# The table of expert blocks, made one piece earlier behind each layer

## The chip, the cores and the metric

The kernel runs on one core of one Trainium2 chip. The metric is the device time of one execution in microseconds (us), and less is better. Several executions are timed and their median is taken; one further execution is recorded by the hardware profiler, and its time is given beside its span.

## The reference

The input is a batch of 8 sequences of 512 tokens with 256 features, all in float32. Four sublayers follow each other, each added to its input behind a layer norm:

```python
x = x + scan_layer(layernorm(x))       # Win, silu, decaying state, Wout
x = x + mixture(layernorm(x))          # 16 routed experts + shared expert
x = x + attention(layernorm(x))        # 16 heads, causal, scores clipped to +-10
x = x + mixture(layernorm(x))          # the same mixture again
```

The mixture is what the change touches. The router gives each token 16 scores (a sigmoid). The 16 experts form 4 groups; the 2 best groups are kept, and in them the 4 best experts. Their weights are normalised and scaled by 2.5. A token's output is the weighted sum of its 4 experts, each `silu(x @ gate) * (x @ up) @ down` with 256 inner features, plus a shared expert of twice that width, which all tokens pass.

## The kernel before

The work has four stages in this order: a stretch for the scan layer, the routed experts of the first mixture, a stretch for attention, and the routed experts of the second mixture.

**A stretch** (`stretch(layer)`) loops over the 8 sequences. Beside the layer's own matmuls for a sequence b it routes sequence b-1 (`Route`: norm, transposes and scores, `choices`) and computes the shared expert of sequence b-2 (`shared_experts`). `choices` is a long chain of small VectorE (DVE) operations: it picks the experts (L558 to L602), counts tokens by expert with two small TensorE (PE) matmuls (`pr`, L609 and L610), works out a row number in DRAM for each choice (L614 to L635) and the weights (L639 to L642), and sends each token's row to its places with 16 indirect DMAs on GpSimd (POOL, L656) into `xg`, where each of the 16 experts has a region of its own.

**Two closing pieces** follow the loop, since routing and shared experts lag behind. The first piece holds the rest of the shared expert of sequence 5 and all of sequence 6's, with the routing of sequence 7. The second holds the shared expert of sequence 7 and the last 8 sends. In a shared expert, L902 is a gate or up matmul (tile `pg`), L919 (first mixture) or L915 (second) its activation on ScalarE (ACT), L920 and L921, or L916 and L917, the two DVE products that make `act`, L930 the down matmul (tile `pd`), L938 its copy out of PSUM on ACT, and L939 its store.

**The table** (`blocks(i, table)`) is what turns the counts into a list of blocks of 128 rows that all belong to one expert. It is a generator of five steps:

1. the regions' ends go to integers (`ends`, L675), SyncE (SP) loads them into registers (L676), and 16 DMAs write zeros behind the regions (L684);
2. the number of blocks by expert, and their sum (`n`, `more`, `nb`, `total`, `many`, L687 to L698);
3. the place of each candidate block in the list (`has`, `ahead`, `also`, `at`, L706 to L717);
4. a 0/1 matrix `chosen` (L721, 128 x 572);
5. 4 + 4 + 4 matmuls that read `chosen` (`pe`, L732, and twice `pl`, L741), a copy on ACT (`expert`, L736), and DVE operations that write the addresses as integers (`spare`, `lines`, L745, L749, L752).

**The routed experts** (`routed`) read the table: each engine loads block addresses from `lines` into registers, SP loads a block's 128 rows (L787), PE transposes them (L802), runs gate and up (`ph`, L813) and down (`pyr`, L841), and POOL adds the rows to the output with an indirect DMA (L850). 136 blocks run in each of the two stages; a branch for more is not taken.

**What sets the order.** `beside(...)` merges several pieces by a share of progress: it always takes a step from the piece that has come the least way. `timed(steps, *places)` gives steps fixed places between 0 and 1 of the merged piece, and after the last place runs what is left of the generator. `spread(a, b, n)` gives n even places. A scheduler then reorders somewhat, so that places are a request and the built order decides; each engine executes its own instructions strictly in the built order, and waits for semaphores.

**PSUM.** In the scan stretch there are 8 banks for all matmul outputs; in the attention stretch 4 for everything but the attention scores (`banks_of(one=4, pair=2)`). A new tile waits until the bank's former tile has been read.

Of the kernel before, what the change touches and what calls it, by code (L numbers as in the profile page):

```python
# [72 lines left out]
def tile_hybrid_block(  # L73
# [61 lines left out]
    def rows_of(part, b: int):  # L135
        return part[b * T : (b + 1) * T, :].rearrange("(t p) d -> p t d", p=P)
# [191 lines left out]
    def timed(steps, *places):  # L328


        def scaled():
            now = 0
            for place in places:
                yield place - now
                now = place
                next(steps)
            for _ in steps:
                pass

        return Piece(1, scaled())  # L340

    def spread(first: float, last: float, many: int):
        return [first + (last - first) * k / many for k in range(many)]

    def some(steps, many: int):

        for _ in range(many):
            yield next(steps)

    def issue(piece):  # L350
        for _ in piece.steps:
            pass


    def turned(src, tag: str, into, copies, home=None):

        rows = src()
        if home is None:
            dst = work.tile([P, KD, T], FP, tag="kb4", name=f"xT_{tag}", bufs=KB)
        else:  # L360
            dst = home(f"xT_{tag}")
        into(dst)
        for k in range(KD):
            pt = bank([P, NT, P], f"pt_{tag}_{k}")
            for t in range(NT):
                nc.tensor.transpose(pt[:, t, :], rows[:, t, k * P : (k + 1) * P], ident)
            flat = pt.rearrange("p t q -> p (t q)")
            copies[k](dst[:, k, :], flat)
            yield T // 2
# [4 lines left out]
    def normed(b: int, tag: str, place, by_vector: bool = False):  # L374

        x_sb = x_tiles[b]
        stats = small.tile([P, NT, 6], FP, tag="stats", name=f"stats_{tag}")
        mv = small.tile([P, NT, 2], FP, tag="mv", name=f"mv_{tag}")
        for t in range(NT):
            nc.vector.bn_stats(stats[:, t, :], x_sb[:, t, :])  # L380
            nc.vector.bn_aggr(mv[:, t, :], stats[:, t, :])
            yield
        rstd = small.tile([P, NT], FP, tag="rstd", name=f"rstd_{tag}")
        if by_vector:


            var = small.tile([P, NT], FP, tag="var", name=f"var_{tag}", bufs=1)
            nc.vector.tensor_scalar(var, mv[:, :, 1], EPS, None, ALU.add)
            bits = small.tile([P, NT], I32, tag="bits", name=f"bits_{tag}", bufs=1)
            nc.vector.tensor_scalar(bits, var.bitcast(I32), 1, None, ALU.logical_shift_right)  # L390
            nc.vector.tensor_scalar(rstd.bitcast(I32), bits, -1.0, HALVED, ALU.mult, ALU.add)
            off = small.tile([P, NT], FP, tag="off", name=f"off_{tag}", bufs=1)
            for _ in range(3):
                nc.vector.tensor_mul(off, rstd, rstd)
                nc.vector.scalar_tensor_tensor(off, off, -0.5, var, ALU.mult, ALU.mult)
                nc.vector.scalar_tensor_tensor(rstd, off, 1.5, rstd, ALU.add, ALU.mult)
            yield
        else:
            nc.vector.tensor_scalar(rstd, mv[:, :, 1], EPS, None, ALU.add)
            nc.gpsimd.tensor_tensor(rstd, rstd, neg_half, ALU.pow)  # L400
        xn = place()
        for t in range(NT):
            nc.vector.tensor_scalar(
                xn[:, t, :], x_sb[:, t, :], mv[:, t, 0:1], rstd[:, t : t + 1], ALU.subtract, ALU.mult
            )
            yield

    def kb4(name: str):
        return work.tile([P, NT, D], FP, tag="kb4", name=name, bufs=KB)
# [762 lines left out]
    def stretch(layer):  # L1172


        i = layer.mixture
        xT, xn, made, routes, sends = {}, {}, {}, {}, []

        def norm(b: int):
            def place():
                xn[b] = kb4(f"xn_{i}_{b}")  # L1180
                return xn[b]

            return normed(b, f"l{i}_{b}", place)

        def turn(b: int):
            return turned(lambda: xn.pop(b), f"l{i}_{b}", lambda xnT: xT.update({b: xnT}), layer.copies)

        def project(b: int):
            made[b], piece = layer.project(b, xT.pop(b))
            return piece  # L1190

        def store(b: int):
            nc.sync.dma_start(out=rows_of(parts[i][0], b), in_=x_tiles[b])

        def experts(b: int):
            return shared_experts(i, b, lambda: routes.pop(b).held["xnT"], i == 1)

        for b in range(layer.ahead):
            if b < layer.early:
                xT[b] = ready.pop(b)  # L1200
            else:
                layer.load(b)
                issue(Piece(0, norm(b)))
                issue(Piece(0, turn(b)))
            if b == 0:
                issue(project(b))
        def start_route(b: int):
            routes[b] = Route(i, b, layer.copies)
            store(b)
            return routes[b]  # L1210

        for b in range(B):
            pieces = [layer.main(b, made.pop(b))]
            nxt, last = b + layer.ahead, b == B - 1
            fill = []
            if layer.ahead > 1 and not last:
                fill.append(project(b + 1))
            if b > 1:
                shared_sum = experts(b - 2)
                if last:  # L1220

                    each = shared_sum.columns // 12
                    rest = Piece((12 - HELD) * each, shared_sum.steps)
                    shared_sum = Piece(HELD * each, some(shared_sum.steps, HELD))
                fill.append(shared_sum)
                pieces.append(timed(sends.pop(), 0.1, 0.14, 0.18, *spread(0.22, 0.66 if last else 0.86, NT * TK)))
            if fill:
                pieces.append(behind(*fill))
            if b > 0:
                r = start_route(b - 1)  # L1230
                pieces.append(timed(r.norm(), *spread(0.0, 0.12, NT), *spread(0.2, 0.28, NT)))
                sends.append(r.rest)
                if last:
                    pieces += [
                        timed(r.scores(), 0.35, 0.38, *spread(0.45, 0.5, NT)),
                        timed(some(r.rest, PICKS), *spread(0.52, 0.66, PICKS)),
                        timed(some(r.rest, 3 + SENT), 0.69, 0.71, 0.73, *spread(0.75, 1.0, SENT)),
                    ]
                else:
                    pieces += [  # L1240
                        timed(r.scores(), 0.42, 0.46, *spread(0.55, 0.6, NT)),
                        timed(some(r.rest, PICKS), *spread(0.66, 0.95, PICKS)),
                    ]
            if nxt < B:
                layer.load(nxt)
                pieces += [
                    timed(norm(nxt), *spread(0.32, 0.44, NT), *spread(0.56, 0.64, NT)),
                    timed(turn(nxt), 0.75, 0.79),
                ]
            issue(beside(*pieces))  # L1250
            if layer.ahead == 1 and nxt < B:
                issue(project(nxt))
        layer.end()

        r = start_route(B - 1)
        chain = 3 + PICKS
        issue(
            beside(  # L1260
                behind(rest, experts(B - 2)),
                timed(r.norm(by_vector=True), *spread(0.0, 0.05, 2 * NT)),
                timed(sends.pop(), *spread(0.0, 0.5, NT * TK - SENT)),
                timed(r.scores(), 0.2, 0.22, *spread(0.28, 0.33, NT)),
                timed(some(r.rest, chain + 8), *spread(0.36, 0.68, chain), *spread(0.7, 1.0, 8)),
            )
        )
        table = []
        issue(
            beside(  # L1270
                experts(B - 1),
                timed(r.rest, *spread(0.0, 0.5, NT * TK - 8)),
                timed(blocks(i, table), 0.03, 0.14, 0.26, 0.38),
            )
        )
        return table

    with banks_of(one=8):
        table = stretch(Scan())
        wqkv_sb, wo_sb = load_attention_weights()  # L1280
# [6 lines left out]
    with banks_of(one=4, pair=2):  # L1287
        table = stretch(Attention())
# [82 lines left out]
```

## Time and profile before

| | |
|---|---|
| median of 3 executions | 1802.87 us (1798.23 to 1807.11) |
| profiled execution: time | 1817.59 us |
| profiled execution: span | 1815.9 us, mean granted PE clock 0.965 |
| PE busy | 1694.6 us, 93% |
| DVE busy | 1088.1 us, 60% |
| ACT busy | 805.3 us, 44% |
| POOL busy | 763.0 us, 42% |
| first closing pieces (scan) | about 321 to 385 us of the span |
| first routed experts | from about 385 to 795 us |
| second closing pieces (attention) | about 1310 to 1377 us |
| second routed experts | about 1377 us to the end |

The span runs from the first to the last instruction of the profiled execution. A row of the timeline gives start, duration, engine, source line, operation, tiles and count; a bracket holds the idle time of that engine just before and what ended it. Matmuls are recorded twice each here, so 2 matmuls are x4. A wait for several semaphores is put down to the one that came last. A few matmul records can be missing, and their ends are modelled.

### The profile page before, as it was taken

Reading aid. Unit: us, or ns where it says so; the run is one execution under the profiler, and the core shown is the slowest. Engines: PE = TensorE matmul, PEld = TensorE weight load, DVE = VectorE, ACT = ScalarE, POOL = GpSimd, SP = SyncE. Lnnn points to the kernel's source line nnn. Section 1 sums busy time; section 2 is a strip of 40 time slices with the busy share of each in tenths; the row PEclk is TensorE's granted clock in tenths of the full one; section 3 lists DMA queues with packets and bytes.
Section 4 is the critical chain, followed back from the end, with each engine's and each line's share of the span. In section 5 each row is a group of like instructions: output and inputs, shape, how many; then the busy total and the mean of one; then the engine's idle time right before and its main releaser. Section 6 shows DMA issues by size and latency. Waiting matters only on the chain. (4 is left out here: it accounts for less than half of the span.)

```text
span 1815.9 us, 32773 instructions
## 1 busy us (share of the span) xinstructions
PE 1694.6 (93%) x10640; PEld 1264.8 (70%) x10640; DVE 1088.1 (60%) x3364; ACT 805.3 (44%) x1740; POOL 763.0 (42%) x665
## 2 busy tenths in 40 slices
PE   5899998889999999989999999999988999999991
PEld 3566665569999999954445545544456999999991
DVE  5877775535555655556776676666643555555552
ACT  2322222125555555545564454454413555555550
POOL 4255554525555655540031321322551555565542
PEclk9899998989999999989999999999998999999995
DMA  5443322525566665540011112122542655566557
GB/s 162 151 149 131 130 78 85 178 77 95 96 97 102 108 97 94 94 88 12 24 58 63 61 64 69 50 72 72 178 147 62 97 97 94 107 118 97 97 105 240
DMA packets 149997, 181.37 MB, mean 100 GB/s; under 512 B 16096, under 2 KB 136960, under 8 KB 149824
## 3 DMA queue, kind: packets, MB, share of 16 engines
q0 software_dynamic: 53136, 76.81, 23.3%
q1 hardware_dynamic: 94320, 96.12, 17.8%
q10 hardware_dynamic: 2368, 6.29, 0.9%
q8 instruction: 89, 1.46, 0.3%
q14 instruction: 84, 0.69, 0.1%
HBM read 81.62 MB, written 97.53 MB: 99 GB/s over the span
## 5 line engine op out<-in xcount | busy, mean ns | idle before, releaser
L850 POOL DMA_INDIRECT part<-rows x272 | 426.4, 1568 | 388.2 <-ACT rows L849 339.9
L656 POOL DMA_INDIRECT xg<-sorted_m,slots_m x256 | 255.4, 998 | 298.2 <-ACT slots_m L653 120.2
L813 PEld LDWEIGHTS ph<-rows,gate 128*128 128x128 f32 x2176 | 286.3, 193 | 16.0 <-ACT rows L803 1.4
L813 PE MATMUL ph<-rows,gate 128*128 128x128 f32 x2176 | 289.7, 276 | 0.6 <-ACT rows L803 0.6
L813 PE MATMUL ph<-rows,up 128*128 128x128 f32 x2176 | 288.5, 276 | 0.0
L841 PE MATMUL pyr<-w_all,rows 128*128 x1088 | 281.9, 381 | 5.4 <-DVE rows L823 3.3
L813 PEld LDWEIGHTS ph<-rows,up 128*128 128x128 f32 x2176 | 266.0, 193 | 0.0
L821 ACT ACTIVATE rows<-ph 128x256 f32<-128x256 f32 x272 | 104.5, 384 | 333.1 <-PE ph L813 330.2
L822 DVE TENSOR_TENSOR rows<-ph,rows 128x256 f32<-128x256 f32 x272 | 115.5, 424 | 202.6 <-ACT rows L821 168.9
L841 PEld LDWEIGHTS pyr<-w_all,rows 128*128 128x128 f32 x1088 | 185.6, 191 | 20.6 <-issue 5.2
L795 ACT COPY gate<-w_all 128x512 f32 x272 | 170.0, 627 | 13.5 <-SPq L883 2.6
L1047 ACT ACTIVATE w_all<-ps_a 128x1024 f32<-128x1024 f32 x128 | 124.4, 1021 | 82.0 <-PE ps_a L1036 69.9
L902 PE MATMUL pg_m<-xT_m,su_sb 128*128 128x512 f32 x256 | 134.4, 650 | 5.2 <-ACT expert_b L736 5.2
L849 ACT ACTIVATE rows<-pyr,gain 128x256 f32<-128x256 f32 x272 | 128.7, 473 | 20.7 <-PE pyr L841 16.9
L795 DVE COPY up<-w_all 128x512 f32 x272 | 118.5, 436 | 32.1 <-PE ph L813 16.2
L1036 PE MATMUL ps_a<-w_all 32*128 32x512 f32 (+3 forms) x1024 | 123.3, 476 | 6.8 <-ACT w_all L1047 5.4
L930 PE MATMUL pd_m<-sd_sb,act_m 128*128 128x256 f32 x512 | 121.8, 386 | 4.5 <-DVE act_m L921 4.5
L902 PE MATMUL pg_m<-xT_m,sg_sb 128*128 128x512 f32 x256 | 123.0, 603 | 0.0
L823 DVE TENSOR_TENSOR rows<-ph,rows 128x256 f32<-128x256 f32 x272 | 115.2, 424 | 8.5
L826 DVE SCALAR_TENSOR_TENSOR gain<-rows,expert_b 128x4 f32<-128x4 f32 x272 | 60.4, 222 | 98.9 <-ACT rows L849 84.9
L802 PE MATMUL pt<-ident,rows 128*128 128x128 f32 x544 | 104.9, 275 | 12.8 <-DMA rows<-xg 12.8
L930 PEld LDWEIGHTS pd_m<-sd_sb,act_m 128*128 128x128 f32 x512 | 96.8, 192 | 27.2 <-DVE act_m L921 5.7
(208 smaller groups left out, 2205.3 us busy)
## 6 DMA issues: line engine op xcount, KB each, us to landing
rows<-xg SPq DMA_DIRECT2D x272, 136.0 KB
part<-x SPq DMA_DIRECT2D x16, 512.0 KB
part<-ys_m SPq DMA_DIRECT2D x16, 512.0 KB
w_all<-in_L_ffn_gate_w_dram SPq DMA_DIRECT2D x24, 256.0 KB
w_all<-in_L_ffn_up_w_dram SPq DMA_DIRECT2D x24, 256.0 KB
w_all<-in_L_ffn_down_w_dram SPq DMA_DIRECT2D x24, 256.0 KB
xg<-zeros SPq DMA_DIRECT2D x34, 136.0 KB
part<-rows POOLq DMA_INDIRECT x272
```

Source lines behind the costliest of these rows:

```text
L656: nc.gpsimd.indirect_dma_start(out=xg[i], out_offset=bass.IndirectOffsetOnAxis(ap=slots[:, at : at + 1], axis=0), in_=rows[:, t, :], in_of ...
L795: copy(here, w_all[:, bass.ds(held[n][0] + half * KD * F, KD * F)])
L813: nc.tensor.matmul(ph[:, s, f * P : (f + 1) * P], lhsT=both[s][:, k * F + f * P : k * F + (f + 1) * P], rhs=rows[:, ROW + k * P : ROW + (k ...
L822: nc.vector.tensor_mul(act, ph[:, 0, :], act)
L823: nc.vector.tensor_mul(act, ph[:, 1, :], act)
L841: nc.tensor.matmul(py, lhsT=act[:, f * P : (f + 1) * P], rhs=w_all[:, bass.ds(w + 2 * KD * F + f * D, D)], start=(f == 0), stop=(f == KF - 1),
L849: nc.scalar.mul(rows[:, 0:D], py, gain[:, TK : TK + 1])
L850: nc.gpsimd.indirect_dma_start(out=parts[i][n % 2], out_offset=bass.IndirectOffsetOnAxis(ap=rows[:, D + 2 * TK : D + 2 * TK + 1].bitcast(U ...
L902: nc.tensor.matmul(dst, lhsT=w[:, k, f * P : (f + 1) * P], rhs=xnT[:, k, :], start=(k == 0), stop=(k == KD - 1),)
L930: nc.tensor.matmul(py[:, j, :], lhsT=acts[n][:, f, t * P : (t + 1) * P], rhs=shared[n][3][:, f, :], start=(n == 0 and f == 0), stop=(n == ...
L1036: nc.tensor.matmul(ps[j // 2][:, j % 2, col : col + n], lhsT=k_sb[w][r, o, c * P : (c + 1) * P], rhs=q_sb[r, o, c * P : T], start=True, st ...
L1047: nc.scalar.activation(es[two], ps[two][:, :, 0:cols], AF.Exp, scale=ATT_SCALE)
```

## The change

The call of `blocks` moves from the second closing piece to the first. Its four places are now 0.66, 0.68, 0.72 and 0.76 of the first piece, with the fifth step right behind the fourth; before they were 0.03 to 0.38 of the second. The 8 steps of the routing chain are placed at 0.36 to 0.64 in place of 0.36 to 0.68, and the first 8 sends from 0.65 on in place of 0.7. The diff applies to both stretches.

```diff
@@ -1256,21 +1256,21 @@
         r = start_route(B - 1)
         chain = 3 + PICKS
+        table = []
         issue(
             beside(
                 behind(rest, experts(B - 2)),
                 timed(r.norm(by_vector=True), *spread(0.0, 0.05, 2 * NT)),
                 timed(sends.pop(), *spread(0.0, 0.5, NT * TK - SENT)),
                 timed(r.scores(), 0.2, 0.22, *spread(0.28, 0.33, NT)),
-                timed(some(r.rest, chain + 8), *spread(0.36, 0.68, chain), *spread(0.7, 1.0, 8)),
+                timed(some(r.rest, chain + 8), *spread(0.36, 0.64, chain), *spread(0.65, 1.0, 8)),
+                timed(blocks(i, table), 0.66, 0.68, 0.72, 0.76),
             )
         )
-        table = []
         issue(
             beside(
                 experts(B - 1),
                 timed(r.rest, *spread(0.0, 0.5, NT * TK - 8)),
-                timed(blocks(i, table), 0.03, 0.14, 0.26, 0.38),
             )
         )
         return table
```

## The prediction

> **What bounds the kernel now.** I read the windows first, to see where PE (TensorE) has idle time at all. The columns are the stretch, its length, busy time of PE, weight load, DVE, ACT and POOL, then PE's clock and the DMA.
>
> ```profile
> 320.00:385.00 65.00, 57.08 (x211) 35.83 (x209) 28.80 (x107) 10.32 (x24) 31.53 (x32) 0.97 0.41 144
> 440.00:760.00 320.00, 319.58 (x2449) 306.96 (x2448) 185.57 (x582) 176.26 (x445) 175.04 (x113) 1.00 0.60 99
> 1310.00:1377.00 67.00, 60.71 (x223) 37.93 (x221) 29.96 (x109) 10.98 (x24) 26.91 (x28) 0.97 0.35 122
> 1400.00:1740.00 340.00, 340.00 (x2609) 327.10 (x2607) 193.15 (x597) 188.08 (x475) 188.40 (x122) 1.00 0.60 100
> ```
>
> In the routed stages (rows two and four) PE is never idle, and a table that is ready earlier cannot make them shorter. The two closing stretches (rows one and three), which alone the change reorders, hold 7.9 and 6.3 us of PE idle time. PE bounds them too, so what counts is how much PE waits there.
>
> The second view is PE's timeline of the attention layer's closing pieces, and the two rows of ACT and DVE that end its longest wait.
>
> ```profile
> 1330.32 1.88 PE L902 MATMUL pg_m<-xT_m,sg_sb 128*128 128x512 f32 x4
> 1333.06 0.43 PE L609 MATMUL pr_m<-sel_m,tri 128*128 128x64 f32 x2 [0.86 <-DVE sel_m L602]
> ...
> 1338.76 7.07 PE L930 MATMUL pd_m<-sd_sb,act_m 128*128 128x256 f32 x32
> ...
> 1354.54 1.25 PE L732 MATMUL pe_b<-chosen_b,cand_e 128*128 128x143 f32 x8
> 1355.72 2.12 PE L741 MATMUL pl_b<-chosen_b,cand_at 128*1 128x143 f32 x16
> 1363.03 3.51 PE L902 MATMUL pg_m<-xT_m,su_sb 128*128 128x512 f32 x4 [5.19 <-ACT expert_b L736]
> ...
> 1383.08 0.66 PE L802 MATMUL pt<-ident,rows 128*128 128x128 f32 x2 [6.20 <-DMA rows<-xg]
> 1362.70 0.28 ACT L736 COPY expert_b<-pe_b 128x143 f32<-128x143 f32 x1 [11.08 <-remote]
> 1362.79 0.29 DVE L745 CAST lines_b<-pl_b 1x143 int32<-1x143 f32 x1 [8.30 <-remote]
> ```
>
> The table costs PE 5.19 us here: three of four banks hold `pe` and the two `pl`, so the next `pg` waits for the copy of `pe`. That copy starts 6.9 us after the end that is recorded for the `pe` matmuls (1355.79). What holds it back the trace does not name. After the wait the four records take 3.51 us where 1.88 is usual: the clock has fallen.
>
> Third, the scan layer's closing pieces:
>
> ```profile
> 325.00 4.11 PE L930 MATMUL pd_m<-sd_sb,act_m 128*128 128x256 f32 x10 [3.88 <-DVE act_m L921]
> 346.51 0.41 PE L609 MATMUL pr_m<-sel_m,tri 128*128 128x64 f32 x2 [2.70 <-DVE sel_m L602]
> 367.99 1.25 PE L732 MATMUL pe_b<-chosen_b,cand_e 128*128 128x143 f32 x8 [0.15 <-issue]
> 378.13 6.31 PE L930 MATMUL pd_m<-sd_sb,act_m 128*128 128x256 f32 x28 [0.63 <-DVE act_m L921]
> 374.69 0.28 ACT L736 COPY expert_b<-pe_b 128x143 f32<-128x143 f32 x1 [9.66 <-PE pg_m L902]
> ```
>
> The copy is late here as well (5.4 us), but with eight banks PE runs on: the table costs it 0.15 us, and about 0.6 us of the last products, which stand behind L745 on DVE.
>
> **The change part by part.** What it does not move: the built order has `ends`, `n`, the register load and the 16 zero DMAs in the first piece already, in both programs (before, L684 issues at 1335.96). On SP only the store of sequence 6's shared expert changes, from ahead of the last zero DMA to behind it, and nobody waits for it near there. POOL's order is unchanged; its first send still waits for the weights (L642), which I put at 1338.8 against 1339.1. The stage's start keeps its chain: last down matmul, copy, store, two register loads on SP, row load, 6.2 us of PE waiting. `lines` was ready 14 us before that and gains nothing by being ready sooner.
>
> (a) Taken away, attention: the 5.19 us wait and the slow matmuls behind it, 3.51 - 1.88 = 1.63 us. Together -6.8.
>
> (b) Taken away, scan: 0.15 + 0.63 = -0.8.
>
> (c) The denser chain. In the built order one gate product, the `pg` pair at 1330.32, now stands behind `pr` instead of ahead of it. DVE's order up to `sel` (L602) is the same, so `pr` waits as late as before while PE has one start-to-start step less to cover it: 1.72 us. Waits of 0.86 and 2.70 us become about 2.6 and 4.4 us: +1.7 each, +3.4. If scores come earlier than in this execution, it is less; between 1.7 and 3.4.
>
> (d) The wait that is added. In the built order PE has, behind `pr`, four gate and up products (4 x 1.72 = 6.9 us with `pr` from 1333.06 to about 1340.5), and then `pe` and `pl`, ahead of all 16 down matmuls of sequence 6. Before, those 16 (7.07 us, at 1338.76) ran without waiting for the table. Now they queue behind matmuls that wait for `chosen`. DVE starts `row` (L614) at 1333.76 and must issue ahead of the end of `chosen`: the counts and places, 2.4 us; the weights, 0.8; `more` to `at`, 3.2; four shared products at 0.6, 2.4; `chosen`, 0.75. These are start-to-start distances from DVE's rows in the same trace. The sum is 9.5, so `chosen` ends at 1343.3, and PE waits 2.8 us. In scan, 347.18 + 9.5 against 353.9 gives 2.8 too. Together +5.6, at least 3.0 if small operations overlap more.
>
> (e) The clock. The row with 3.88 us of idle is followed by ten records in 4.11 us, which at the rate of the 7.07 us row (0.22 each) need 2.2: 1.9 us lost. The row with 2.70 us of idle is followed by `pg` in 1.94 us: nothing lost. So the 4.4 us of (c) in scan costs +1.9, and the waits of 2.6 and 2.8 us cost nothing; if 2.8 is over the edge, 2 x 1.9 more.
>
> [...]
>
> (f) The late copy stays: ACT's copy of `pe` now stands ahead of the copies of sequence 6's down outputs, and the second down tile needs its bank. `pe` ends at about 1344.6, the copy comes 6.9 us later at 1351.5, PE gets there at 1343.3 + 1.25 + 2.1 + 3.5 = 1350.1: +1.4 in attention, 0 if the copy is prompt. Scan has banks enough: 0.
>
> (g) The first 14 blocks of each routed stage have gate copies, products and gains in another order on ACT and DVE, and the steady order is the same. PE has almost no idle there (0.24 and 0.30 us rows at the start), so I take 0, bounded by -0.5 and by four blocks that lose a gate copy's 0.6 us: +2.4 a stage, +4.8.
>
> Sum: -6.8 - 0.8 + 3.4 + 5.6 + 1.9 + 1.4 = +4.7 us. The profiled execution took 1817.6 us, which gives 1822.3. That execution is 14.7 us above the median of the plain runs, 1802.87; if the difference carries over, the median is 1807.5, 0.26% slower. About 0.5% (9 us) is what a measurement of this kernel can tell from no change, so this is no change.
>
> The lower bound: (c) 1.7, (d) 3.0, (e) and (f) zero, (g) -1 (twice -0.5): -3.9, or 1799. The upper: (e) with three cold waits, 5.7, (g) 4.8, and (a) zero, because plain runs might lack the late copy (then (f) is zero too): +18.7, or 1821.5.
>
> **The rivals.**
>
> *The added waits go cold.* One mechanism: PE's queue holds `pe` ahead of the down matmuls, and DVE's chain in front of `chosen` runs 1.7 us longer than I add up, in each stretch, because products of the shared expert wait for ACT in between. It decides once the chain is 1.1 us longer, since from 3.9 us of waiting on the clock has fallen. Price: 2 x (1.7 + 1.9) = 7.2 on top of 4.7, 1814.8, slower. For it: DVE has stalls of 0.4 us before single products in the same stretch. Against it: its inputs are ready in my sum. That plain runs lack the late copy, so that (a) and (f) fall away, ends near it: 1807.5 + 6.8 - 1.4 = 1812.9.
>
> *The table hides completely.* If `chosen` is ready when PE arrives, (d), (e) and (f) vanish: -6.8 - 0.8 + 3.4 = -4.2, 1798.7; with (c) at its low end 1797. Against it: DVE works without a pause from `row` to `chosen`, 2.8 us longer than PE.
>
> *The change does less than it says.* The scheduler pulled half of the table forward already; if gains and waits cancel, the time stays at 1803.
>
> **How the numbers follow.** Forecast, small net waits: 0.45, at 1807.5, its own range 1803 to 1811. Cold waits or no late copy before: 0.27, at 1813 to 1815. Hidden table: 0.13, at 1798. Cancelling: 0.15, at 1803. The medians of three runs scatter by some 4 us (1798.23 to 1807.11), which widens the ends to 1797 and 1817. Slower by over 0.5% is above 1811.9: most of the second case and a little of the first, 0.30. Faster by over 0.5% is below 1793.8: no case reaches it without scatter, 0.08. The rest, 0.62, is no change.
>
> **What would show each step.** (a) No PE row of several us that ACT's L736 ends in the attention stretch. (c) `pr` rows with waits of about 2.6 and 4.4 us. (d) `pe` rows that wait about 2.8 us for DVE's `chosen`, ahead of L930. (e) Slow rows behind the scan layer's `pr` only. (f) A wait of some 1.4 us inside L930 for L736. The row load's wait of 6.2 us stays, and so does PE without idle time in the routed stages. I am wrong if the routed stages change length, if POOL's sends end later than the last store, or if `pe` does not wait.

## The result, and the profile after

The kernel after takes 1808.57 us (median of 20 executions, 1804.46 to 1815.39); the kernel before takes 1800.16 us beside it (20 executions, 1797.06 to 1807.11). The ratio is 1.0045, 95% interval 1.0035 to 1.0055: 8.1 us slower by the ratio, 8.4 us between the medians. That is a small loss, and a clear one; it lies inside the 0.5% that I called no change. The forecast was 1807.5.

The profiled execution of after, the longest of its 20, took 1815.39 us with a span of 1813.7 us. That is 2.2 us shorter than the span that the prediction started from, while the timed executions are 8.1 us longer. The experiments explain most of it: in three of four sets of runs the kernel before took 1800.2 to 1801.4 us, in the other 1815.2 us, and its first profile (1817.6 us) belongs to the upper level while all the plain times were at the lower. So the profiles of before and after that a reader would compare first are not of the same kind, and every ratio below is within one set. Where a run's cost is given in us, it is the difference of the medians, which can lie up to 1.5 us from what the ratio gives.

The windows of after, columns as in the prediction:

```profile
320.00:385.00 65.00, 57.24 (x212) 36.38 (x210) 25.55 (x93) 10.94 (x23) 31.23 (x33) 0.97 0.42 148
440.00:760.00 320.00, 318.71 (x2440) 305.88 (x2439) 184.28 (x580) 174.59 (x441) 173.97 (x113) 1.00 0.59 99
1310.00:1377.00 67.00, 57.99 (x216) 36.90 (x214) 27.86 (x100) 12.88 (x27) 25.10 (x26) 0.97 0.34 120
1400.00:1740.00 340.00, 339.98 (x2604) 326.56 (x2603) 193.35 (x593) 187.68 (x476) 186.79 (x122) 1.00 0.59 100
```

Rows two and four say that the routed stages are as full as before, to 1 us. Rows one and three show 7.8 and 9.0 us without PE work, but the closing pieces end at 382.2 and 1372.5 here, so 2.8 and 4.5 us of that already belong to the wait for the first row load. Windows at fixed times slide over a stage that ends earlier; the waits must be read one by one.

PE's timeline of after in the attention stretch, and ACT's row of the copy:

```profile
1330.34 0.43 PE L609 MATMUL pr_m<-sel_m,tri 128*128 128x64 f32 x2 [2.58 <-DVE sel_m L602]
1339.82 2.17 PE L732 MATMUL pe_b<-chosen_b,cand_e 128*128 128x143 f32 x8 [1.90 <-DVE chosen_b L721]
1341.92 2.81 PE L741 MATMUL pl_b<-chosen_b,cand_at 128*1 128x143 f32 x16
1378.60 0.66 PE L802 MATMUL pt<-ident,rows 128*128 128x128 f32 x2 [6.13 <-DMA rows<-xg]
1342.03 0.28 ACT L736 COPY expert_b<-pe_b 128x143 f32<-128x143 f32 x1 [5.19 <-PE pe_b L732]
```

`pr` waits 2.58 us, `pe` waits 1.90 us, and `pe` and `pl` run at the lower clock (2.17 and 2.81 us; the prediction's rows have 1.25 and 2.12). The copy of `pe` is prompt: `pe` ends at 1341.99. (The 5.19 in its bracket is ACT's own idle time, and no PE row of this profile waits for that copy; that it equals PE's wait in the profile before is chance.) The wait for the first row load is as it was. The scan stretch of after:

```profile
341.69 0.41 PE L609 MATMUL pr_m<-sel_m,tri 128*128 128x64 f32 x2 [0.88 <-DVE sel_m L602]
351.15 1.25 PE L732 MATMUL pe_b<-chosen_b,cand_e 128*128 128x143 f32 x8 [1.91 <-DVE chosen_b L721]
352.43 0.28 ACT L736 COPY expert_b<-pe_b 128x143 f32<-128x143 f32 x1 [4.28 <-PE pe_b L732]
```

The same two waits, 0.88 and 1.91 us, without slow rows behind them, and again a prompt copy.

### The profile page after: what moved, and what is told of

Read it like the earlier page. It is cut to its first block, busy times and chain, and to the rows that moved or that the text cites. A ratio compares the mean times of both kernels' runs of the same rounds, so it can differ in the third digit from the quotient of the medians.

```text
span 1813.7 us, 32770 instructions
## 1 busy us (share of the span) xinstructions
PE 1696.4 (94%) x10640; PEld 1267.5 (70%) x10640; DVE 1088.5 (60%) x3364; ACT 804.7 (44%) x1740; POOL 760.1 (42%) x665
## 5 line engine op out<-in xcount | busy, mean ns | idle before, releaser
L813 PEld LDWEIGHTS ph<-rows,gate 128*128 128x128 f32 x2176 | 286.8, 193 | 16.1 <-ACT rows L803 1.7
L813 PE MATMUL ph<-rows,gate 128*128 128x128 f32 x2176 | 290.1, 277 | 0.6 <-ACT rows L803 0.6
L813 PE MATMUL ph<-rows,up 128*128 128x128 f32 x2176 | 289.3, 276 | 0.6 <-DVE up L795 0.6
L813 PEld LDWEIGHTS ph<-rows,up 128*128 128x128 f32 x2176 | 266.5, 193 | 1.0 <-DVE up L795 1.0
L795 ACT COPY gate<-w_all 128x512 f32 x272 | 170.1, 627 | 14.0 <-SPq L883 2.6
L795 DVE COPY up<-w_all 128x512 f32 x272 | 117.0, 431 | 25.7 <-ACTq L883 14.1
L802 PE MATMUL pt<-ident,rows 128*128 128x128 f32 x544 | 104.7, 275 | 12.6 <-DMA rows<-xg 12.6
```

The lines of the kernel that those rows point to most:

```text
L795: copy(here, w_all[:, bass.ds(held[n][0] + half * KD * F, KD * F)])
L802: nc.tensor.transpose(pt[:, k, :], rows[:, k * P : (k + 1) * P], ident)
L813: nc.tensor.matmul(ph[:, s, f * P : (f + 1) * P], lhsT=both[s][:, k * F + f * P : k * F + (f + 1) * P], rhs=rows[:, ROW + k * P : ROW + (k ...
```

## The experiments

The theory, from these rows: each of the waits is paid once, at its length, and the late copy that the prediction counts as a gain was never in the plain runs of that set. The sum is (2.58 - 0.86) + 1.90 + (2.17 - 1.25) + (2.81 - 2.12) = 5.2 us in attention and 0.88 + 1.91 = 2.8 us in scan, 8.0 in all. The rivals: half of the change does it all, or the table's place in the order costs by itself.

### The kernel before, once more

Nothing is edited; what this run adds is a second profile of before.

> The kernel before, unchanged, to see whether the late copy of its first profile is there always. Theory W (the plain runs of the kernel before lack the late copy, and the change costs what PE waits for): no wait of several us on the copy L736 in the attention stretch, the copy within 0.1 us of the end of the pe matmuls in both stretches, the pr wait 0.9 us in attention and none in scan, span about 1800 to 1805 us, ratio 1.000. Theory L (the late copy is a fixed part of the kernel before, and the loss came from elsewhere, such as the new order of the first routed blocks): again 5 to 7 us between pe and its copy in both stretches, and 5 us of PE waiting.

Measured: 1800.8 us, ratio 0.9997 (0.9987 to 1.0006), span 1802.5. The timeline of this profile, three rows of PE and one of ACT:

```profile
324.39 2.02 PE L366 MATMUL pt_m<-ident,sorted_m 128*128 128x128 f32 x8 [1.44 <-DVE sorted_m L403]
341.38 0.33 PE L609 MATMUL pr_m<-sel_m,tri 128*128 128x64 f32 x2
1325.79 0.43 PE L609 MATMUL pr_m<-sel_m,tri 128*128 128x64 f32 x2 [0.86 <-DVE sel_m L602]
364.05 0.28 ACT L736 COPY expert_b<-pe_b 128x143 f32<-128x143 f32 x1 [4.22 <-PE pe_b L732]
```

In scan `pr` does not wait at all (2.70 us in the first profile), `pe` ends at 364.01 and is copied 0.04 us later (5.4 us later in the first profile), and in attention no PE row waits for L736. This is the base that the timed runs of before have. The rows that only the first profile shows are the waits of 3.88, 2.70, 0.63 and 5.19 us and 1.9 + 1.63 us of slow clock, 15.9 us. This one has 1.44 us elsewhere in scan (before `pt_m`, L366) that the first has not, and slow rows behind it: `pt_m` takes 2.02 us (1.04 in the first profile) and the 16 `pd` records that follow take 4.97 (3.62), 2.3 us together from start to start. The difference, 12.2 us, is most of the 13.4 us between the two spans and of what separates the levels, 1815.2 - 1800.5 = 14.7; the rest stays open.

### The denser chain alone

```diff
-  timed(some(r.rest, chain + 8), *spread(0.36, 0.68, chain), *spread(0.7, 1.0, 8)),
+  timed(some(r.rest, chain + 8), *spread(0.36, 0.64, chain), *spread(0.65, 1.0, 8)),
   ...
   timed(blocks(i, table), 0.03, 0.14, 0.26, 0.38),   # stays in the second piece
```

> Only the denser routing chain and earlier sends; the table stays in the second piece. Theory W: one gate product less ahead of pr, so pr waits 2.6 us in attention (0.9 before) and 0.9 in scan (0 before): +2.6 us, ratio 1.0014, and no wait of pe. Rival (the denser chain carries the loss): +8 us, 1.0045.

Measured: 1803.39 us, ratio 1.0012 (1.0003 to 1.0020), +2.9 us. `pr` waits 0.91 us in scan and 2.6 in attention, 0.9 and 1.7 more than in the run above: 2.6 us. `pe` does not wait.

### The table alone

```diff
   timed(some(r.rest, chain + 8), *spread(0.36, 0.68, chain), *spread(0.7, 1.0, 8)),
+  timed(blocks(i, table), 0.66, 0.68, 0.72, 0.76),    # first piece
   ...
-  timed(blocks(i, table), 0.03, 0.14, 0.26, 0.38),    # second piece
```

> Only the table moves to the first piece; chain and sends are placed as before. Theory W: pr has its gate product ahead of it again, but one product less lies between pr and pe, so what pr gains pe loses: waits of 0.9 and 3.6 us in attention, 0 and 2.8 in scan, with a slow clock behind at least the first; +7 to +9 us, ratio 1.004 to 1.005, the same as the whole change. Rival (the two edits add up): +5.5 us, 1.003.

Measured: 1812.67 us, ratio 1.0061 (1.0045 to 1.0078), +12.1 us, more than the 7 to 9 that I expected: by the medians, half of the change costs more than the whole (the two intervals overlap a little). PE's timeline shows why:

```profile
349.66 1.25 PE L732 MATMUL pe_b<-chosen_b,cand_e 128*128 128x143 f32 x8 [3.69 <-DVE chosen_b L721]
350.84 3.78 PE L741 MATMUL pl_b<-chosen_b,cand_at 128*1 128x143 f32 x16
1334.94 2.28 PE L732 MATMUL pe_b<-chosen_b,cand_e 128*128 128x143 f32 x8 [3.68 <-DVE chosen_b L721]
1337.14 3.93 PE L741 MATMUL pl_b<-chosen_b,cand_at 128*1 128x143 f32 x16
```

With the old spacing PE reaches `pe` sooner after `pr`, so both waits are 3.7 us, and both have slow rows behind them: `pl` loses 1.66 and 1.81 us, `pe` 1.03 us in attention. 3.69 + 3.68 + 1.66 + 1.81 + 1.03 = 11.9. So within the change the denser chain is no loss: it gives PE one more gate product to run ahead of `pe`, which shortens a wait of 3.7 us, with slow rows behind it in both stretches, to one of 1.9 us, in the two profiles of after without them in scan, and in one of the two in attention.

### The whole change, with the table's matmuls later

```diff
-  timed(blocks(i, table), 0.66, 0.68, 0.72, 0.76),
+  timed(blocks(i, table), 0.66, 0.68, 0.72, 0.76, 0.985),
```

The fifth step (L732 to L752) now stands behind the down matmuls of sequence 6; everything else is as in the kernel after.

> The whole change, but the table's fifth step (the pe and pl matmuls and what follows them) is placed at 0.985 of the first piece, so that PE has all 16 down matmuls of sequence 6 ahead of it. Theory W: the waits of pe (1.9 us in each stretch) and the slow clock behind one of them (1.6 us) go, the pr waits stay: +2.6 us over the kernel before, ratio 1.0014, 5.4 us less than the whole change. Theory L (loss in the routed stages or elsewhere): stays at +8 us, 1.0045.

Measured: 1803.92 us, ratio 1.0016 (1.0004 to 1.0028), +3.4 us. `pe` starts without a wait in both stretches, here in attention, straight behind the down matmuls:

```profile
1335.01 1.14 PE L732 MATMUL pe_b<-chosen_b,cand_e 128*128 128x143 f32 x8
```

The two `pr` waits (0.9 and 2.6 us) are left. Of the 8.4 us, some 5 belong to the table's matmuls standing ahead of 7 us of work that does not need the table.

### Old chain, late matmuls

The first piece has the table with the fifth step at 0.985, and the chain keeps 0.36 to 0.68. This kernel ran in two sets. First at the upper level:

> The table's first four steps stand in the first piece as in the kernel after, its matmuls (pe, pl) at 0.985 of that piece, and the chain keeps its old, looser spacing. Theory (each wait of TensorE is paid once, at the wait's own length, and nothing else of the change costs): pr's waits go back to 0 in scan and 0.86 us in attention, pe has no wait, so the time is that of the kernel before: ratio 1.000 (0.999 to 1.001). Rival (the move of the table costs by itself: its vector operations crowd the chain, or the copies hold a bank): as the kernel with the whole change and late matmuls showed 3.4 us, of which the two pr waits explain 2.6, 1 to 3 us would be left here: ratio 1.0006 to 1.0017.

Measured: 1825.95 us against 1815.2, ratio 1.0062 (1.0044 to 1.0079), far from 1.000. Then at the lower level:

> The same kernel as the one with the old chain and the table's matmuls at 0.985. Theory: where before takes about 1800.5 us, nothing is read late, neither pr nor pe waits more than before: ratio 1.000 (0.999 to 1.001). Where before takes about 1815 us: again 1.006 (1.004 to 1.008), as the two copies of lines_b in VectorE's queue come late there. Rival (the late matmuls cost by their place alone): 1.003 to 1.006 at both levels.

Measured: 1801.08 us against 1801.44, ratio 1.0001 (0.9991 to 1.0012), with `pr` waits of 0 and 0.86 us and none for `pe`. So the earlier table is free when nobody waits for it, and it gains nothing either. In the upper level's profile two DVE operations that write `lines` come late instead, and PE waits for them in attention:

```profile
1357.98 1.98 PE L902 MATMUL pg_m<-xT_m,sg_sb 128*128 128x512 f32 x4 [1.45 <-DVE lines_b L745]
1366.40 3.78 PE L902 MATMUL pg_m<-xT_m,su_sb 128*128 128x512 f32 x4 [6.44 <-DVE lines_b L752]
```

### One stretch at a time

The whole change for `i == 0` alone, then for `i == 1` alone. Both ran at the upper level.

> The whole change in the scan layer alone; attention as before. Theory: pr waits 0.9 us and pe 1.9 us in scan, no slow rows there, attention as before: +2.8 us, ratio 1.0016 (1.0008 to 1.0024). Rival (the cost is the same in both stretches, half of the measured 8.1 us): +4.05 us, ratio 1.0022.

Measured: 1819.43 us, ratio 1.0020 (1.0007 to 1.0033), +4.2 us. This decides nothing: the theory's range and the rival's 1.0022 both fit. The rows are not those of the theory either, for `pr` waits 3.30 us at this level, with slow rows behind it, and `pe` 1.64.

> The whole change in the attention layer alone; scan as before. Theory: pr waits 2.6 us in place of 0.86, pe 1.9 us, and pe and pl run 0.9 and 0.7 us longer on the slower clock behind these: +5.2 us, ratio 1.0029 (1.002 to 1.0038). Rival (half of the whole cost): +4.05 us, ratio 1.0022. The profile decides more sharply than the ratio: pe's eight matmuls at about 2.2 us in attention and 1.25 us in scan by the theory.

Measured: 1824.06 us, ratio 1.0057 (1.0038 to 1.0075), +8.9 us. The size does not carry over from the lower level (5.2 us). `pe` is not slow here; `pr` and the `pg` behind it are, and lose 1.7 us (0.43 and 1.94 us are usual). With the waits that makes 5.3 us, and the rest of the 8.9 stays open. The shape is the telling part. ACT's timeline of the attention-only kernel, and PE's rows:

```profile
1344.77 0.28 ACT L736 COPY expert_b<-pe_b 128x143 f32<-128x143 f32 x1 [4.26 <-issue]
1363.45 0.58 ACT L938 COPY ys_m<-pd_m 128x512 f32<-128x512 f32 x1 [7.95 <-remote]
1332.35 0.69 PE L609 MATMUL pr_m<-sel_m,tri 128*128 128x64 f32 x2 [2.58 <-DVE sel_m L602]
1333.26 3.18 PE L902 MATMUL pg_m<-xT_m,sg_sb 128*128 128x512 f32 x4
1364.09 3.78 PE L902 MATMUL pg_m<-xT_m,su_sb 128*128 128x512 f32 x4 [5.05 <-ACT ys_m L938]
```

The copy of `pe`, moved 18 us forward, is prompt; but at the place in the last piece where it used to be late, another copy is late now, and PE waits 5.05 us for that one, with a slow row behind it. With the late `lines` above, these are two profiles in which the late reads stay in the last piece whatever stands there; by them, the late reads belong to a place in the stretch at the upper level and not to the table, and taking one reader away gains nothing.

### The kernel after, once more

> The kernel after, unchanged. Two levels of the kernel before have been seen: about 1800.5 us, with TensorE's results read as soon as they are there, and about 1815 us, with some of them read 3 to 7 us late near the end of each stretch. Theory: where before takes about 1800.5 us, the waits of pr and pe are paid in full as in the first comparison: ratio 1.0045 (1.0035 to 1.0055). Where before takes about 1815 us, the late reads stay in attention and find another reader: in the last piece TensorE still waits about 5 us for a copy (of ys_m, no longer of expert_b), and the sum of the scan-only and attention-only runs is paid: ratio 1.007 (1.005 to 1.009). Rival (the prediction's step on the late copy): at the upper level the 5.2 us wait goes with the moved copy: ratio 1.000 to 1.003.

Measured: 1809.12 us against 1801.44, ratio 1.0042 (1.0028 to 1.0056), +7.7 us. The waits are the same (0.92, 1.90, 2.58, 1.90), but `pe` in attention is at full clock in this profile:

```profile
1336.60 1.25 PE L732 MATMUL pe_b<-chosen_b,cand_e 128*128 128x143 f32 x8 [1.90 <-DVE chosen_b L721]
```

So of the theory's 8.0 us, 6.4 are in both profiles of after and 1.6 in one of two. The upper level was not met, and what the whole change costs there stays open.

### What can be had: the row load ahead of the store

All profiles so far show PE idle for about 6.1 us at each routed stage's start, and name the DMA of the rows. The table is ready long before that in either kernel. This kernel is the one before; only the loads of the first two blocks' rows (L787) move, into the second closing piece at 0.9, with their row numbers' registers on SP.

```diff
   timed(blocks(i, table), 0.03, 0.14, 0.26, 0.38),
+  timed(first_two(i, table), 0.9, 0.92),      # load(0), load(1): SP alone
...
-  load(first); load(first + 1)
+  if first: load(first); load(first + 1)
+  else: weights(first)                        # registers of PE, ACT and DVE
```

It ran in two sets, at the upper and then the lower level.

> The kernel before, with the loads of the first two routed blocks' rows (L787) issued in the second piece at 0.9, behind the table and ahead of the last store of that stretch in SyncE's queue, and their row numbers alone loaded there; nothing else is moved. It asks what the finished table can be used for: in all traces so far TensorE stands 6.1 to 6.4 us at each routed stage's start, and the trace names the DMA rows<-xg. Theory (that wait is the transfer behind the last store in the queue; next late are the branch and the copies of the first expert's weights): the idle shrinks from about 6.2 to some 2 to 3 us in both stages, 6 to 8 us in all: ratio 0.996 (0.995 to 0.998). Rival (the stop is the branch on the count of blocks and the loads of registers behind it, which every engine goes through, and the rows only come in last): the idle stays above 5 us, ratio 0.999 to 1.000.

Measured: 1809.43 us against 1815.2, ratio 0.9968 (0.9951 to 0.9985), 5.8 us faster.

> The same kernel as the one with the first two loads of rows issued ahead of the stretch's last store. Theory (a wait on the path is worth its length at either level of before): 5.8 us less, ratio 0.9968 (0.996 to 0.9976). Rival (the gain was part of the late reads of the upper level, such as the expert_b wait, which was 2.4 us there in place of 5.2): at the lower level 0.998 to 0.9995.

Measured: 1795.34 us against 1801.44, ratio 0.9958 (0.9946 to 0.9971), 6.1 us faster, a little more by the ratio than I expected: the first version that beats before, at both levels. PE's timeline of the second run, scan (L827, L828 and L838 are L802, L803 and L813 of before):

```profile
379.99 0.63 PE L827 MATMUL pt<-ident,rows 128*128 128x128 f32 x4 [1.21 <-PEq L781]
382.75 1.16 PE L838 MATMUL ph<-rows,gate 128*128 128x128 f32 x8 [2.13 <-ACT rows L828]
```

The wait for the DMA is gone, 1.2 us for the branch and the registers remain (0.9 in attention), and next late is ACT's copy of the turned rows, which three copies of expert weights precede (1.66 us in ACT's timeline of the first run). The last kernel puts that copy first:

```diff
-  fetch(first)
   turn(first)
+  fetch(first)
```

and holds the first three gate copies and the first two copies of turned rows in program order.

> Early rows as in the run beside it, and ScalarE copies the first block's turned rows (L830, pt) ahead of the three copies of experts' weights, held in program order. In the trace of early rows TensorE waits 2.45 and 2.24 us for that copy at the two stages' starts, while three gate copies of 0.55 us run ahead of it. Theory: the wait falls by about 1 us in each stage, as one gate copy has still to come in before ph: ratio 0.9957 (0.995 to 0.9968). Rival (the pinned order delays a later gate or rows copy by as much): 0.9968 to 0.998.

Measured: 1788.67 us against 1801.44, ratio 0.9927 (0.9914 to 0.9940), 12.8 us faster, where I expected 7.7. The idle time explains only part. The rest goes with the clock, here in windows of the first 22 us behind the last down matmul in scan (each begins within half a us of its end), for the kernel before (the run once more):

```profile
378.00:400.00 22.00, 15.51 (x99) 14.16 (x98) 7.30 (x26) 8.65 (x20) 2.51 (x2) 0.84 0.33 89
```

for early rows at the lower level:

```profile
379.00:401.00 22.00, 18.58 (x131) 17.61 (x132) 9.56 (x34) 10.92 (x27) 4.81 (x3) 0.92 0.36 89
```

and for the last kernel, with PE's two waits (L829 and L842 are L802 and L813, L820 is L795):

```profile
378.00:400.00 22.00, 19.60 (x150) 18.07 (x150) 10.48 (x38) 12.10 (x29) 6.26 (x4) 1.00 0.43 101
```

```profile
378.98 0.66 PE L829 MATMUL pt<-ident,rows 128*128 128x128 f32 x4 [0.83 <-ACTq L915]
380.86 1.16 PE L842 MATMUL ph<-rows,gate 128*128 128x128 f32 x8 [1.21 <-DVE up L820]
```

The granted clock (third column from the end) goes 0.84, 0.92, 1.00, and the PE records that are through after 22 us go 99, 131, 150. In attention it is 0.84, 0.84, 1.00 and 106, 123, 155. At the full rate, 157 records in the following 20 us of the kernel before or 0.127 us each, the last kernel's lead over before is (51 + 49) x 0.127 = 12.7 us, the measured 12.8; for early rows (32 + 17) x 0.127 = 6.2, the measured 6.1. So the whole gain arises in these two windows.

The rows divide it. PE's waits in the first three blocks of the two stages add up to 13.1 us in the kernel before, 7.1 with early rows and 4.8 in the last kernel. The slow `pt` and `ph` rows behind them cost about 4.8, 4.7 and 0 us (a group of eight `ph` records takes 0.89 us from start to start at the full rate, and up to 1.87 here). So early rows gain 6.0 us of idle time and almost nothing by the clock; the last kernel gains 8.3 us of idle time and 4.8 by the clock, 13.1 in all.

## Why the prediction came out right, and where it was wrong

The time and its side of the bound were right; several of its steps were not, and their errors cancel. That the time came within 1.1 us is in part luck: the change was forecast at +4.7 us and came at +8.4 between the medians, and the base of the forecast, the median of three executions, was 1802.87 us where 20 give 1800.16, so that 2.7 us of the base made up for most of what the sum lacks. Nor is 0.5% what can be told from no change: with 20 executions of each kernel the interval is 0.1% to either side. By its terms, for the timed runs:

| step | predicted | measured |
|---|---|---|
| (a) copy wait and slow clock gone, attention | -6.8 | 0: not in the base |
| (b) the same, scan | -0.8 | 0: not in the base |
| (c) `pr` waits longer | +3.4 | +2.6 (1.72 and 0.88); alone +2.9 timed |
| (d) `pe` waits for `chosen` | +5.6 | +3.8 (1.90 and 1.91) |
| (e) slow clock | +1.9 in scan | 0 in scan; 1.6 in attention in one of two profiles |
| (f) copy holds the down tile's bank | +1.4 | 0 |
| (g) first routed blocks reordered | 0 | no wait seen |
| sum | +4.7 | +6.4 to +8.0; timed +8.4 and +7.7 between the medians |

**The step that failed is the frame of the sum.** It carried the 14.7 us between the profiled execution and the plain runs over as a constant. That difference was itself made up in large part of the rows in (a) and (b) and the 2.70 us in (c), so they could not be gained from runs that did not have them. The warning stood in the text: plain runs "might lack the late copy", as part of the second case, with 1812.9. In mechanism that case was the right one. Its terms (c), (d) and (e) add up to 10.9, where 6.4 to 8.0 came, and it kept the 0.8 of (b); with the measured sizes it gives 1802.9 + 6.4 to 8.0, 1809 to 1811.

**(f), and (a) at the upper level.** I expected the late copy to move with the matmuls. In the one profile that has the whole change in attention at that level it did not: moved forward, it is prompt, and where it had been a different copy is late. That corrects (a) a second time, since even where the wait exists it does not go away.

**(c)** is right in attention (2.6 forecast, 2.58 measured). In scan 4.4 was forecast, and 0.88 came, because the 2.70 us it started from were a product of the upper level; without them one gate product less ahead of `pr` uses up slack first.

**(d)** is right in kind, 0.9 us too long each. The chain from `row` to the end of `chosen` takes from 1331.04 to 1339.77, 8.7 us, where I added 9.5: the four shared products stand in it as forecast, and the small operations follow each other more closely than in the rows from which I took their distances.

**(e)** is wrong in where the slow clock sits, because it read a limit out of two rows: 2.70 us of waiting had cost nothing, 3.88 us had. No such limit is in the runs. In after's first profile the slow rows came behind 2.58 and 1.90 us of waiting within 12 us, in the second run of before behind 1.44 us, and the very `pr` wait that was free in the first profile is not free where old chain and late matmuls ran at the upper level, though it is shorter there:

```profile
345.31 0.41 PE L609 MATMUL pr_m<-sel_m,tri 128*128 128x64 f32 x2 [1.84 <-DVE sel_m L602]
345.78 3.45 PE L902 MATMUL pg_m<-xT_m,su_sb 128*128 128x512 f32 x4
```

In attention `pe` waits 1.90 us for `chosen` in both profiles of after. Behind that wait the granted clock reads 0.50 in slices of 1 us from 1340 to 1343 us in the first profile, and `pe` and `pl` take 2.17 and 2.81 us; in the second the same records take 1.25 and 2.12 us, as in the profile before. So behind the same wait one program had slow rows in one execution and none in another. What decides it, no run shows.

**The table hidden completely** did not happen in the kernel after, but can be built: old chain and late matmuls, ratio 1.0001. It shows that a hidden table is worth nothing. The rival's own case, with the denser chain, is the whole change with late matmuls: +3.4 us, of which the `pr` waits of (c) are 2.6, in place of -4.2, again for want of (a) and (b).

What caused the late reads at the upper level stays open. They occur in all five profiles of that level and in none of the other nine, the trace names no holder, and no kernel was tried that provokes them.

## What to carry to other kernels

Before a wait is booked as a gain, ask whether the timed runs have it: a profiled execution 0.8% above the median of the plain runs is made of rows, and the rows that make it are the ones not to count. Matmuls that wait for a table belong behind work that does not need it (here +3.4 us in place of +8.4), and making a result earlier gains only as far as its consumer is issued earlier too, here the first load in SP's queue (ratio 1.0001 for the earlier table, 0.9958 for the earlier load). At a stage's start PE's pause can count twice, once as idle time and once as slow clock behind it (13.1 and about 4.8 us in the kernel before), and the second part need not shrink with the first: early rows cut the pauses to 7.1 us and kept 4.7 us of slow clock.

## What the runs showed of the hardware

The kernel before, unchanged, has two levels 14.7 us apart (0.8%), and the timed executions of a set stay on one of them (1796.78 to 1807.11 us in three sets, 1812.00 to 1823.77 in the other); its first profile was at the other level than the timed executions beside it. The chip alone does not set the level, as the record names the same chip for the set at the upper level (1815.2 us) and the last set at the lower (1801.44). The upper can be told from the DMA issues of a profile: with the kernel before at the upper level the line of the row loads has no time to landing,

```profile
rows<-xg SPq DMA_DIRECT2D x272, 136.0 KB
```

and with the same kernel at the lower level it has one:

```profile
rows<-xg SPq DMA_DIRECT2D x272, 136.0 KB, 2.5
```

The line is without a time in all five profiles of the upper level and has 2.5 in all nine of the lower. The slow clock at a stage's start cost about 4.8 us beside 13.1 us of idle time in the kernel before, over both stages. Cutting the pause from 6.1 us to 1.2 and 2.1 us around 0.63 us of work in scan (0.9 and 2.2 in attention) left the clock at 0.92 (0.84) over the 22 us from the last down matmul on, and cutting it to 0.8 and 1.2 us (0.9 and 0.9) kept it at 1.00. In these runs the length of a pause does not tell alone whether slow rows follow: 1.44 and 1.84 us were followed by them (granted clock 0.66 in the 5 us from 325 and from 345 us), 2.70 us was not (1.00 from 345 to 352 us).
